# A relational graph attention layer with 23 instead of 24 buffers of gathered keys and values

## The chip, the cores and the metric

The kernel runs on one core of a Trainium2 chip. The metric is the device time of one execution in microseconds. Three runs took 1737.93, 1730.97 and 1749.97 us, median 1737.93.

## The reference

3125 nodes with 128 features and 100,000 edges, sorted by destination, each of one of five relations. For each relation every edge gets a query of its destination and a key and a value of its source (eight heads of 16), the attention is a softmax over the edges of one destination and one relation, and the weighted values are summed over edges and relations:

```
for r in range(5):
    mask = edge_types == r
    q = einsum(x[dst], W_Q[r]); k = einsum(x[src], W_K[r]); v = einsum(x[src], W_V[r])
    logits = (q * k).sum(-1) / 4 + attn_bias[r]
    m = segment_max(where(mask, logits, -1e9), dst)
    e = where(mask, exp(logits - m[dst]), 0)
    out += segment_sum(e / (segment_sum(e, dst)[dst] + 1e-12) * v, dst)
h = out @ out_proj_w.T + out_proj_b + x
y = x + layernorm(h) * ln_gamma + ln_beta
result = layernorm(y)
```

## The kernel before

**Tables.** A first stage (until some 120 us) multiplies the nodes by the five relations' weights and writes a table of keys and values to memory, `kv_d`, one row of 256 floats (1 KB) per node and relation. Queries go to `q_d`. A second path for inputs that don't fit the assumptions is compiled behind a test and not run.

**Groups and steps.** The edges are cut into 196 groups of 512, four edges on each of 128 partitions. A loop of steps k, written out in full with the order fixed by hand (lines 1123 to 1229), treats several groups at once at different points of their way. The first half of a group g runs in step g:

- `gather(g)`, line 698: four indirect DMAs issued by GpSimd, each 128 rows of `kv_d` into one of the four slots of the buffer `kvs_[g % KVB]`, with KVB = 24. Five groups (3, 6, 9, 12, 15) fetch their sources' features instead and multiply them on TensorE.
- `spread_q` (L803, TensorE) brings the queries of the group's window of nodes to its edges with 12 weight loads and 12 matmuls against a one-hot matrix `hot`.
- `logits` (L816 and L817, VectorE) multiplies queries by the gathered keys and sums per head; `store_logits` sends the logits to memory, `lg_d`.

**Maxima.** The nodes lie in 25 blocks of 128. When the last group that can hold an edge of a block has been through `logits` (about every eighth group), the step after issues `maxima_load` (L829): one indirect DMA on GpSimd, which fetches the logits of each node's edges out of `lg_d` into `ell`. It waits until the logits it needs have landed. `maxima` (L844 to L888: ScalarE once, then VectorE, in the steps three and four after that load's last group) makes the maxima, which go to memory and come back per group as `mw`.

**The second half** of group v runs in step `at_k[v]`, which the code works out from the blocks: v + 16 for the first seven groups, v + 18 for the next 15, v + 19 for all others. `spread_m` (L920, TensorE) brings the maxima to the edges, `less_max` (L929, VectorE) and `exps` (L933, ScalarE) make the exponentials, `weigh` (L938, VectorE) multiplies the gathered values by them, `sums` (L972, L974, L981, TensorE) adds over the edges of a node with a second one-hot matrix `at`. `norm` (L993 to L996, VectorE) divides, and projection, layer norms and output follow per block.

**Buffers.** The weighing is the last reader of a group's keys and values. So with 24 buffers the first DMA of `gather(g)` waits until VectorE has done `weigh` of group g - 24. The pool `hold` has 21 buffers of `hot` and `lg`, which live from before `logits` to `less_max`.

**Queues.** Each engine takes its instructions in the order of the program. In step k the program has, for GpSimd, `gather(k + 3)` and then, if a block is full, `maxima_load`; no other work stands on GpSimd in this part. Nothing ties GpSimd to a step but its waits: for the buffer, for the DMA that used the same semaphore eight DMAs ago, and, at L829, for the stored logits. In the last 16 steps the program has `gather(k + 1)` there. On VectorE a step is `weigh`, `less_max` of the next group, `norm`, `logits`, the one-hot matrix (L794), then maxima or layer norms where due. On TensorE it is `spread_m` of the next group, `sums`, `spread_q` of the next group.

Of the kernel before, what the change touches and what calls it, by code (L numbers as in the profile page):

```python
# [53 lines left out]
AHEAD = 3  # L54
# [6 lines left out]
SPAD = 5  # L61
XG = range(3, 16, 3)
QB = 3
KVB = 24
KVA = 9


# [1 line left out]
def gnn_kernel(  # L69
# [19 lines left out]
    with tc.manual_schedule():  # L89
        windowed_path(  # L90
            tc, n_bad_i, x, src, dst, edge_type, w_q, w_k, w_v, attn_bias, out_w, out_b,
            gamma, beta, out,
        )
# [39 lines left out]
def windowed_path(  # L133
# [5 lines left out]
    ctx = ExitStack()  # L139
# [34 lines left out]
    def buffers(those):  # L174
        for i in those:
            kvs_[i] = ctx.enter_context(tc.tile_pool(name=f"kvp{i}", bufs=1)).tile(
                [P, T, KVW], F32, name=f"kv{i}"
            )
# [508 lines left out]

    ps = ctx.enter_context(tc.tile_pool(name="ps", bufs=2, space=PSUM))
    buffers(i for i in range(KVB) if i not in at_once)
    hold = ctx.enter_context(tc.tile_pool(name="hold", bufs=KVB - AHEAD))  # L690
    flow = ctx.enter_context(tc.tile_pool(name="flow", bufs=2))
    late_flow = ctx.enter_context(tc.tile_pool(name="late_flow", bufs=2))
    def gather(g):
        if g in XG:
            return
        kv = kvs_[g % KVB]
        for t in range(T):
# [61 lines left out]
    def turn_x(g):  # L759
        xe = kvs_[g % KVB][:, :, H:]  # L760
        tx = ps.tile([P, T, P], F32, name="tx", tag="me")
        for t in range(T):
            nc.tensor.transpose(tx[:, t, :], xe[:, t, :], ident)
        live["tx", g] = tx
# [24 lines left out]
    def put_kv(g, t0):  # L789
        nc.scalar.copy(kvs_[g % KVB][:, t0 : t0 + 2, :], live.pop(("pk", g, t0)))  # L790

# [21 lines left out]
    def logits(g):  # L813
        kv, lg = kvs_[g % KVB], live["lg", g]
        prod = flow.tile([P, T, H], F32, name="prod", bufs=1)
        nc.vector.tensor_tensor(prod, kv[:, :, :H], live.pop(("qe", g)), op=ALU.mult)  # L816
        nc.vector.tensor_reduce(  # L817
            lg[:, :, :HEADS], prod.rearrange("p t (k d) -> p t k d", d=HD), AX.X, ALU.add
        )
# [915 lines left out]
```

## Time and profile before

| | |
|---|---|
| runs (median; lowest to highest) | 1737.93 us; 1730.97 to 1749.97 |
| profiled execution: device time | 1728.01 us |
| its span, first to last instruction | 1726.5 us |
| mean granted TensorE clock | 0.706 |
| PE busy (matmuls), PEld (weight loads) | 1030.0 us, 774.3 us |
| VectorE, ScalarE, GpSimd busy | 944.9, 640.4, 797.9 us |
| software queue (gathers, L829): share of 16 DMA engines | 22.5%, 112.08 MB |
| SP's hardware queue | 21.3%, 85.12 MB |

Times in a line of the timeline are the start and the duration in us, then engine, line, operation, the tiles written and read, how often, and in brackets the idle time before it on its engine and what ended it. "issue" means that the engine waited for nothing that the profile shows; "remote" and "another core or an unknown queue" that the profile can't name the releaser. GpSimd's "busy" counts the time in which it prepares and issues a DMA, not the transfer.

### The profile page before, as it was taken

How to read it: one execution, taken by the hardware profiler on the slowest of the kernel's cores; microseconds unless marked ns; L12 is line 12 of the kernel's file. 1: busy time of each engine (PE TensorE's matmuls, PEld its weight loads, DVE VectorE, ACT ScalarE, POOL GpSimd, SP SyncE). 2: the span in 40 equal slices, each digit the busy share in tenths (PEclk: the TensorE clock that was granted, in tenths of full speed). 3: DMA queues.
4: the chain of work that ended last, by engine and by line, in shares of the span. 5: the costliest groups of instructions: out<-in, count | busy, mean ns of one | idle time of the engine just before them, and what ended most of it. 6: DMA issues, size and time to landing. Idle time of an engine off the chain costs nothing.

```text
span 1726.5 us, 26128 instructions
## 1 busy us (share of the span) xinstructions
PE 1030.0 (60%) x7746; PEld 774.3 (45%) x7746; DVE 944.9 (55%) x2536; ACT 640.4 (37%) x2258; POOL 797.9 (46%) x901
## 2 busy tenths in 40 slices
PE   6874745345555546656755655665576556554676
PEld 2443524334444434434534544454454445443554
DVE  3552536345545554654754666466466646544776
ACT  1540103134334334333523434344343434442544
POOL 6344243355445445445454555536455553644300
PEclk8886966567667677666766666667676666757778
DMA  6773425245335445445544544544454443544410
GB/s 160 265 272 93 103 85 112 75 118 130 101 96 135 102 112 133 104 103 137 126 103 118 127 116 124 134 105 126 117 126 121 122 135 84 137 113 107 98 27 14
DMA packets 181946, 203.66 MB, mean 118 GB/s; under 512 B 83943, under 2 KB 146819, under 8 KB 181676
## 3 DMA queue, kind: packets, MB, share of 16 engines
q0 software_dynamic: 40576, 112.08, 22.5%
q1 hardware_dynamic: 136790, 85.12, 21.3%
q10 hardware_dynamic: 4430, 4.71, 1.1%
q8 instruction: 64, 1.05, 0.2%
q14 instruction: 86, 0.70, 0.1%
HBM read 166.51 MB, written 35.28 MB: 117 GB/s over the span
## 4 chain that ended last, share of the span: by engine, by line
PE 27%; DVE 27%; issue 18%; another core or an unknown queue 14%; ACT 5%; DMA 2%; SPq 1%; POOL 1%; DVEq 0%; ACTq 0%
PE pp L972 8%; PE qe L803 4%; DVE wl L867 4%; DVE mx L873 4%; DVE prod L816 4%; PE me L920 4%; PE pk L781 3%; DVE lg L817 3%; DVE wv L938 2%; PE pp L974 2%; PE pr L403 2%; ACT at L958 2%; DVE hot L794 2%; PE prq L724 1%
## 5 line engine op out<-in xcount | busy, mean ns | idle before, releaser
L698 POOL DMA_INDIRECT kv<-kv_d,idx x764 | 725.6, 950 | 503.0 <-DVE den L993 271.4
L972 PE MATMUL pp<-wv,at 128*125 128x136 f32 x1568 | 382.2, 374 | 83.6 <-issue 75.3
L972 PEld LDWEIGHTS pp<-wv,at 128*125 128x125 f32 x1568 | 286.7, 247 | 167.8 <-issue 159.1
L803 PE MATMUL qe<-qw,hot 125*128 125x128 bf16 x2352 | 228.9, 253 | 109.7 <-issue 98.3
L920 PE MATMUL me<-mw,hot 125*128 125x64 bf16 (+1 forms) x2352 | 142.3, 214 | 210.0 <-issue 110.5
L803 PEld LDWEIGHTS <-hot 125*128 125x128 bf16 x2352 | 197.6, 123 | 126.9 <-issue 112.1
L929 DVE TENSOR_TENSOR me<-lg,me 128x32 f32<-128x32 f32 x196 | 37.6, 192 | 374.6 <-remote 202.2
L958 ACT ACTIVATE at<-row_at,nkey 128x125 f32<-128x125 f32 x744 | 237.6, 398 | 0.0
L933 ACT ACTIVATE me<-me 128x32 f32<-128x32 f32 x196 | 35.7, 182 | 537.2 <-DVE me L929 451.2
L920 PEld LDWEIGHTS <-hot 125*128 125x128 bf16 x2352 | 123.4, 112 | 241.4 <-issue 191.4
L938 DVE TENSOR_TENSOR wv<-kv,me 128x512 f32<-128x512 f32 x196 | 132.9, 678 | 139.7 <-remote 85.9
L829 POOL DMA_INDIRECT ell<-lg_d,start_i x25 | 23.7, 946 | 303.2 <-DMA lg_d<-lg 87.3
L816 DVE TENSOR_TENSOR prod<-kv,qe 128x512 f32<-128x512 f32 x196 | 132.9, 678 | 43.6 <-PE qe L803 27.6
L974 PE MATMUL pp<-pt,carried 125*5 125x136 f32 x390 | 97.8, 339 | 68.4 <-issue 34.1
L817 DVE TENSOR_REDUCE lg<-prod 128x32 f32<-128x512 f32 x196 | 134.5, 686 | 6.8
L1006 ACT COPY oT<-pp 128x25 f32 x196 | 33.9, 173 | 245.6 <-remote 85.5
L961 ACT ACTIVATE at<-at 128x500 f32<-128x500 f32 (+1 forms) x196 | 117.4, 599 | 6.2
L724 PE MATMUL prq<-wq,xTq 128*128 128x384 f32 (+1 forms) x88 | 54.5, 718 | 94.3 <-DVE hot L794 77.8
L781 PE MATMUL pk<-wkv,xm 128*128 128x256 f32 x200 | 63.2, 447 | 50.7 <-issue 46.2
L867 DVE TENSOR_TENSOR wl<-by_head,shut 128x1536 f32<-128x1536 f32 (+2 forms) x49 | 73.1, 1491 | 36.0 <-PE pk L781 27.6
L981 PEld LDWEIGHTS pp<-rsum,o 125*128 125x128 f32 x392 | 80.5, 246 | 23.0 <-issue 22.2
L981 PE MATMUL pp<-rsum,o 125*128 125x25 f32 x392 | 71.9, 262 | 20.7 <-issue 16.1
(191 smaller groups left out, 1203.4 us busy)
## 6 DMA issues: line engine op xcount, KB each, us to landing
kt<-key_d SPq DMA_DIRECT2D x196, 128.0 KB
qw<-q_d SPq DMA_DIRECT2D x196, 96.0 KB
kv_d<-kvs SPq DMA_DIRECT2D x24, 640.0 KB
kv<-kv_d,idx POOLq DMA_INDIRECT x764
q_d<-q SPq DMA_DIRECT2D x22, 480.0 KB
lg_d<-lg SPq DMA_DIRECT2D x196, 18.0 KB
mw<-m_d SPq DMA_DIRECT2D x196, 6.0 KB
xr<-in_x SPq DMA_DIRECT2D x24, 64.0 KB
```

Of the source, the lines that this page charges most:

```text
L698: nc.gpsimd.indirect_dma_start(out=kv[:, t, :], out_offset=None, in_=kv_d[:, :], in_offset=bass.IndirectOffsetOnAxis(ap=idx[:, t, g : g + ...
L803: nc.tensor.matmul(qe[:, t, :], hot[:, t, :], qw[:WR, s, :], start=(s == 0), stop=(s == 2))
L816: nc.vector.tensor_tensor(prod, kv[:, :, :H], live.pop(("qe", g)), op=ALU.mult)
L817: nc.vector.tensor_reduce(lg[:, :, :HEADS], prod.rearrange("p t (k d) -> p t k d", d=HD), AX.X, ALU.add)
L867: nc.vector.tensor_tensor(wl, by_head[:, None].to_broadcast([P, n, nh, D]), shut[:, :n, None, :].to_broadcast([P, n, nh, D]), op=ALU.add,)
L920: nc.tensor.matmul(me[:, t], hot[:, t, :], mw[:WR, None, :, s, :].to_broadcast([WR, times, 2, HEADS // 2]), start=(s == 0), stop=(s == 2),)
L938: nc.vector.tensor_tensor(wv[:, :, :H].rearrange("p t (k d) -> p t k d", d=HD), kv[:, :, H:].rearrange("p t (k d) -> p t k d", d=HD), live ...
L958: nc.scalar.activation(at[:, t, :], row_at[:, :WR], AF.Abs, bias=nkey[:, t, g : g + 1], scale=1.0)
L961: nc.scalar.activation(at[:, on_dve:], at[:, on_dve:], AF.Relu, bias=1.0, scale=-1.0)
L972: nc.tensor.matmul(pp, at[:, t, :], wv[:, t, :], start=(t == 0), stop=(t == T - 1))
L974: nc.tensor.matmul(pp[:R], carried[:WR, g, :], live.pop(("pt", g - 1)), start=False, stop=False,)
L981: nc.tensor.matmul(op, live.pop(("o5", done)), rsum[:WR], start=True, stop=True)
```

## The change

The number of buffers of keys and values is 23, and the pool `hold`, whose size was worked out from it (24 - 3), keeps its 21.

```diff
-KVB = 24
+KVB = 23
+HELD = 21
 KVA = 9
...
     buffers(i for i in range(KVB) if i not in at_once)
-    hold = ctx.enter_context(tc.tile_pool(name="hold", bufs=KVB - AHEAD))
+    hold = ctx.enter_context(tc.tile_pool(name="hold", bufs=HELD))
```

Every use of a buffer (`gather`, `turn_x`, `put_kv`, `logits`, `weigh`) takes it as `kvs_[g % KVB]`. The first DMA of `gather(g)` so waits for `weigh` of group g - 23. No instruction is added, removed or put in another place of its engine's order.

## The prediction

> **What bounds the kernel now.** I read the page first: shares by engine, the chain that ended last, the costliest groups.
>
> ```profile
> PE 27%; DVE 27%; issue 18%; another core or an unknown queue 14%; ACT 5%; DMA 2%; SPq 1%; POOL 1%; DVEq 0%; ACTq 0%
> ...
> L698 POOL DMA_INDIRECT kv<-kv_d,idx x764 | 725.6, 950 | 503.0 <-DVE den L993 271.4
> ...
> L929 DVE TENSOR_TENSOR me<-lg,me 128x32 f32<-128x32 f32 x196 | 37.6, 192 | 374.6 <-remote 202.2
> ```
>
> No engine is full, and a third of the chain is "issue" or waits the profile can't name. GpSimd waits 271 us for VectorE: that is a gather waiting for its buffer (the line named, L993, follows the weighing, L938, on VectorE; the gather starts 0.3 us after the weighing ends). Does anyone wait for gathered data? From the view of line 816, the first reader, what ended VectorE's idle time before it:
>
> ```profile
>   DMA kv<-kv_d,idx: 0.6, 1
> ```
>
> Once, 0.6 us in 196 groups. So gathers are early enough; the question is what else they do. Next, the timeline. The starts of L816 show steps of 3 to 7.5 us, and about every eighth group one of some 22 us. Here is one, on GpSimd, TensorE and VectorE in turn:
>
> ```profile
> 920.69 0.95 POOL L829 DMA_INDIRECT ell<-lg_d,start_i  x1 [6.71 <-DMA lg_d<-lg]
> 921.94 0.95 POOL L698 DMA_INDIRECT kv<-kv_d,idx  x1 [0.30 <-issue]
> ...
> 940.75 0.94 POOL L698 DMA_INDIRECT kv<-kv_d,idx  x1 [0.30 <-issue]
> ```
> ```profile
> 939.05 0.26 PE L803 MATMUL qe<-qw,hot 125*128 125x128 bf16 x1 [1.12 <-issue]
> 940.44 0.27 PE L803 MATMUL qe<-qw,hot 125*128 125x128 bf16 x1 [1.13 <-issue]
> ...
> 944.64 0.58 PE L803 MATMUL qe<-qw,hot 125*128 125x128 bf16 x4 [1.11 <-issue]
> ```
> ```profile
> 927.17 0.68 DVE L938 TENSOR_TENSOR wv<-kv,me 128x512 f32<-128x512 f32 x1
> 944.84 0.20 DVE L929 TENSOR_TENSOR me<-lg,me 128x32 f32<-128x32 f32 x1 [16.98 <-remote]
> ```
>
> GpSimd was held 6.7 us at the load of logits (L829) and then issued 17 DMAs without a pause, one per 1.25 us. From 7 us into that run until 2 to 3 us after its end TensorE gets its instructions at multiples of 0.7 us ("issue": it waits for nothing recorded), and VectorE stands still for 17 us behind it. The same in busy time, columns PE, PEld, DVE, ACT, POOL, granted clock, DMA share, GB/s:
>
> ```profile
> 917.00:927.00 10.00, 7.34 (x89) 6.33 (x87) 8.65 (x27) 9.30 (x28) 4.79 (x6) 0.92 0.71 175
> 927.00:945.00 18.00, 4.83 (x21) 2.67 (x20) 1.02 (x5) 0.35 (x2) 11.34 (x12) 0.50 0.42 114
> ```
>
> The DMA engines are less busy in the stall (0.42) than before it (0.71), so it is not bandwidth. What tracks it is the run's length. In the GpSimd timeline I took as a run all issues with pauses under 0.6 us, and beside each summed TensorE's gaps over 0.6 us between starts, until 3 us after its end. Past 400 us: runs of 8 have 2.1 to 3.5 us of gaps, the two of 12 have 9.2 and 11.0, the eight of 13 have 12.4 to 14.2, the eleven of 17 have 18.8 to 20.9. Runs of 8 and 12 hold no load of logits, so that load is not the cause. Each further group (four DMAs) costs some 5 us. The trace gives a comparison for nothing, since runs after the load have 13 or 17 issues:
>
> ```profile
> 983.86 0.95 POOL L829 DMA_INDIRECT ell<-lg_d,start_i  x1 [6.84 <-DMA kt<-key_d]
> ...
> 998.88 0.95 POOL L698 DMA_INDIRECT kv<-kv_d,idx  x1 [0.30 <-issue]
> 1003.35 0.95 POOL L698 DMA_INDIRECT kv<-kv_d,idx  x1 [3.52 <-DVE den L993]
> ```
>
> This run stopped after three groups, because the fourth's buffer was not free. From one such load to the next: after 17 issues 62.6 us (mean of nine, 482 to 1286 us; 57.8 to 64.3), after 13 issues 58.4 us (five, 984 to 1401 us; 56.7 to 59.9). One more run of 13, at 736 us, was followed after 2.1 us by the next gather and took 64.0.
>
> **The change, part by part.** Instructions and their order stay as they are on all five queues; HELD keeps the hold pool at 21. What moves is one wait: the first gather of group g waited for the weighing of g-24, now g-23. In the steady part group v is weighed in step v+19, so a gather may start from step g-4 instead of g-5.
>
> The added wait, priced. Behind it on GpSimd stand the group's other three DMAs, the next groups, and every eighth group L829. Setting each gather to 0.3 us after the weighing it now waits for, with all else as traced, 110 of the 172 from group 24 on start later. Landing is 2.3 to 3.8 us after a group's last issue (bytes of the software queue counted in order). Slack from landing to L816 has a median of 31 us for groups 44 to 186 and becomes 26; the smallest in the steady part is 15.8. At the end groups 192 to 194 keep 11.0, 8.0 and 7.7, and 195 keeps its 1.2, since L829 holds it in both. Cost on the path: nothing, covered by these 8 to 30 us; if the cover failed, 5 us per group. L829's data land 3 us after issue and are read 26 us later (947 us), so up to 5 us of delay there is covered too.
>
> The DMA page of the Trainium skill (DMA: Bandwidth & Descriptors, Rules for kernel authors) speaks against the change: issue a DMA early, wait late. By that rule the sum could only be a loss, up to 5 us a group; the 0.6 us of L816 shows that this kernel is far past the point where earlier helps.
>
> What it saves. At a load of logits in step k, today's backlog is group k+4 (free since step k-1), then k+5, k+6, k+7 as weighings in steps k, k+1, k+2 end before the stall catches VectorE. With 23, k+7 needs the weighing of step k+3, behind the stall. In the run above, groups 102, 103 and 104 find buffers at 919.3, 922.3 and 927.9, but 105 only at 952.5. The eleven runs of 17 become 13: 11 x (62.6 - 58.4) = 46 us. Three longer early or late runs (33 at 283 us, 21 at 355 and 1575) lose one group by the same arithmetic: 3 x 5.0 = 15 us. The eight runs of 13 would become 9, but the moved group falls into the pause before L829: group 109, issued at 972.3, moves to 978.7 to 983.4 and meets the load at 983.9, so the run begins 5 us earlier and again has 13 issues. I take nothing there; bounds are 8 x 5 gained, or 2 us each lost because a 4-run stands 1.7 us before it (pauses of 1.6 and 1.2 us at 398 and 436 us left 2.7 and 3.5 us of gaps). Sum: about 60 us.
>
> The clock page (TensorE: Matmul & The Clock Gate, HAM oscillation) would blame the half clock that follows an idle array. The rows show 0.50 in the stall, but 12 matmuls of L803 take 0.83 us at full clock and 1.46 at half, against 9 us here; by that rule a shorter stall saves at most some 0.6 us x 22, 14 us in all.
>
> The profiled execution took 1728.0 us (span 1726.5), 10 below the median of the runs shown, 1737.9. 1728 - 60 = 1668 for such a run, 1678 on the median.
>
> **Rivals.** (a) *No change.* The stall is not caused by the run, or the same issues cost the same wherever they lie, and the group moved ahead of L829 gives all of it back. For it: the 64.0 us period, and 1.7 us pauses may not count as pauses. Against: TensorE's gaps begin some 6 us into a run and end within 3 us of its end, whatever its content. Time 1738, give or take 15.
>
> (b) *Slower.* Between the stall and the next load, gathers stand as 4, 4+4 and 4 issues with pauses of 2.3 to 2.8 us, which keep TensorE fed. Buffers freed one by one under 5.3 us apart would close them: an 8 becomes a 12, and gaps grow from 3 to 10 us, 7 per period. Nine such periods use up the 60 us, eleven or more show as a loss, all 20 make 140 - 60 = +80: 1818. For it: 12-runs at 1439 and 1501 us, in the faster steps at the end. Against: those pauses come from the maxima steps (7 us on VectorE), which stay.
>
> (c) *More than forecast.* All 22 loads lose a group outright, 110 us: 1628.
>
> (d) The change does nothing: excluded, as 110 gathers would have to wait longer.
>
> **How the numbers follow.** Forecast (3 to 4%) with what lies towards (c) 0.70, (a) 0.15, (b) 0.15. Runs of this kernel spread over 19 us, so 1%, 17 us, is what a measurement can tell: faster 0.70, same 0.15, slower 0.15. Range: 1635 leaves out the last of (c), 1750 takes in (a) and leaves out most of (b), about 2 in 10 together; without the rivals I would say 1655 to 1705.
>
> **What would show it.** After L829, 13 issues or fewer in every run, where 17 stood; L929's "remote" well below 202 us and the longest L816 steps near 16 us, not 22; 58 us from load to load; L816 still waiting under 5 us for gathers; GpSimd's wait on VectorE before L698 above 271. Wrong if runs of 17 remain across L829, if 12-runs appear between loads, or if the steps stay at 22 us with shorter runs.

## The result and the profile after

| | before | after |
|---|---|---|
| median of 4 runs each (lowest to highest) | 1739.14 us (1730.97 to 1749.97) | 1663.74 us (1658.07 to 1668.21) |
| profiled execution: device time, span | 1728.01, 1726.5 us | 1665.20, 1663.5 us |
| mean granted TensorE clock | 0.706 | 0.724 |

The ratio is 0.956, 95% interval 0.950 to 0.962: 75 us less, where 60 were forecast. (The two profiled executions differ by 63 us: the one before was quicker than its other runs.) That is so where these runs were taken. On two other chips the kernel before takes some 1220 us, and on the one of them where the changed kernel ran too, both take the same; the fifth experiment is about that.

Line numbers after the change are one higher (L698 is L699). The page and the groups by line of the changed kernel, for the lines that were shown of before:

```profile
PE 29%; DVE 28%; issue 19%; another core or an unknown queue 10%; ACT 5%; DMA 2%; SPq 1%; DVEq 0%; ACTq 0%; POOL 0%
...
L699 POOL DMA_INDIRECT kv<-kv_d,idx x764 | 724.5, 948 | 587.9 <-DVE den L994 346.6
...
L930 DVE TENSOR_TENSOR me<-lg,me 128x32 f32<-128x32 f32 x196 | 37.7, 193 | 348.6 <-remote 195.6
```

GpSimd's idle time behind VectorE before the gathers went from 271 to 347 us: the added wait. No reader of gathered data pays for it: the view of line 817, the first reader of gathered data, still has one wait:

```profile
  DMA kv<-kv_d,idx: 0.5, 1
```

L930's "remote" hardly moved (202.2 to 195.6 us), although its longest stalls shrank. The time went out of unnamed waits (the chain's share of them is 10% instead of 14%) and out of waits spread over other lines (L939's "remote" fell from 85.9 to 63.2 us).

Now a load of logits in the timeline. It is the same load of the program that stood at 983.86 us before, and the nearest in time to the one at 920.69 us. The bracket gives the idle time before the line on its engine:

```profile
925.01 0.95 POOL L699 DMA_INDIRECT kv<-kv_d,idx  x1 [0.30 <-issue]
926.71 0.94 POOL L830 DMA_INDIRECT ell<-lg_d,start_i  x1 [0.75 <-issue]
927.96 0.95 POOL L699 DMA_INDIRECT kv<-kv_d,idx  x1 [0.30 <-issue]
...
936.71 0.95 POOL L699 DMA_INDIRECT kv<-kv_d,idx  x1 [0.30 <-issue]
944.70 0.94 POOL L699 DMA_INDIRECT kv<-kv_d,idx  x1 [7.04 <-DVE den L994]
```
```profile
934.09 0.59 PE L804 MATMUL qe<-qw,hot 125*128 125x128 bf16 x4 [0.69 <-issue]
935.52 0.26 PE L804 MATMUL qe<-qw,hot 125*128 125x128 bf16 x1 [0.84 <-issue]
...
938.36 0.37 PE L804 MATMUL qe<-qw,hot 125*128 125x128 bf16 x2 [1.62 <-issue]
```
```profile
928.44 0.69 DVE L939 TENSOR_TENSOR wv<-kv,me 128x512 f32<-128x512 f32 x1 [1.72 <-PE me L921]
939.94 0.20 DVE L930 TENSOR_TENSOR me<-lg,me 128x32 f32<-128x32 f32 x1 [10.82 <-remote]
```

GpSimd issues the load and then two groups, nine issues, and stops for want of a buffer; before, three groups followed this load. The group ahead of it, 109, now ends 0.75 us before it instead of 6.85. TensorE's trickle is the same as before (gaps that end in "issue"), but shorter: 10 us of gaps in the run instead of 14. VectorE stands still for 10.8 us, where two stalls of 6.0 and 6.7 us stood at this load. At the load that had the stall of 17.0 us (at 920.69 us, now at 873.00), 8 gathers follow instead of 16, and the longest stall is 5.2 us.

Counted as in the prediction (a run ends at a pause of 0.6 us or more; beside it TensorE's gaps over 0.6 us between starts of matmuls or weight loads, until 3 us after its end), from 400 us on:

| | before | after |
|---|---|---|
| issues in a run that holds a load of logits | 11 x 17, 8 x 13, 1 x 21 | 2 x 17, 5 x 13, 12 x 9, 1 x 5 |
| TensorE gaps in the runs that hold a load | 354 us | 197 us |
| runs of 8 or more without a load; gaps in them | 17; 63 us | 26; 113 us |
| TensorE gaps in runs of 4 | 136 us | 170 us |
| mean time of eight groups, group 44 to 164 | 61.2 us | 58.6 us |

(The last two loads, in runs of five issues and one, are left out of the first line. Seven of the runs of 9 and one of 13 begin with the group that stands ahead of the load.) So 157 us of gaps went from the loads, and 83 of them came back in other runs.

### The profile page after: what moved, and what is told of

Read it like the earlier page. It is cut to its first block, busy times and chain, and to the rows that moved or that the text cites. A ratio compares the mean times of both kernels' runs of the same rounds, so it can differ in the third digit from the quotient of the medians.

```text
span 1663.5 us, 26129 instructions
## 1 busy us (share of the span) xinstructions
PE 1043.0 (63%) x7746; PEld 790.5 (48%) x7746; DVE 945.4 (57%) x2536; ACT 638.7 (38%) x2258; POOL 796.5 (48%) x901
## 4 chain that ended last, share of the span: by engine, by line
PE 29%; DVE 28%; issue 19%; another core or an unknown queue 10%; ACT 5%; DMA 2%; SPq 1%; DVEq 0%; ACTq 0%; POOL 0%
PE pp L973 9%; PE qe L804 4%; PE me L921 4%; DVE wl L868 4%; DVE mx L874 4%; DVE prod L817 4%; PE pk L782 3%; DVE wv L939 3%; DVE lg L818 2%; PE pp L975 2%; PE pr L404 2%; ACT at L959 2%; DVE hot L795 2%; PE prq L725 1%
## 5 line engine op out<-in xcount | busy, mean ns | idle before, releaser
L699 POOL DMA_INDIRECT kv<-kv_d,idx x764 | 724.5, 948 | 587.9 <-DVE den L994 346.6
L973 PE MATMUL pp<-wv,at 128*125 128x136 f32 x1568 | 392.7, 385 | 43.3 <-issue 34.1
L973 PEld LDWEIGHTS pp<-wv,at 128*125 128x125 f32 x1568 | 295.7, 256 | 122.4 <-issue 116.0
L804 PE MATMUL qe<-qw,hot 125*128 125x128 bf16 x2352 | 229.9, 256 | 87.7 <-issue 77.6
L804 PEld LDWEIGHTS <-hot 125*128 125x128 bf16 x2352 | 203.3, 125 | 99.6 <-issue 86.3
L921 PEld LDWEIGHTS <-hot 125*128 125x128 bf16 x2352 | 126.6, 113 | 253.5 <-issue 197.0
L934 ACT ACTIVATE me<-me 128x32 f32<-128x32 f32 x196 | 35.7, 182 | 542.0 <-DVE me L930 409.5
L930 DVE TENSOR_TENSOR me<-lg,me 128x32 f32<-128x32 f32 x196 | 37.7, 193 | 348.6 <-remote 195.6
L939 DVE TENSOR_TENSOR wv<-kv,me 128x512 f32<-128x512 f32 x196 | 133.0, 679 | 104.0 <-remote 63.2
L817 DVE TENSOR_TENSOR prod<-kv,qe 128x512 f32<-128x512 f32 x196 | 132.9, 678 | 43.2 <-PE qe L804 25.7
L975 PE MATMUL pp<-pt,carried 125*5 125x136 f32 x390 | 101.4, 350 | 57.8 <-ACT pt L988 27.4
```

Of the source, the lines that this page charges most:

```text
L699: nc.gpsimd.indirect_dma_start(out=kv[:, t, :], out_offset=None, in_=kv_d[:, :], in_offset=bass.IndirectOffsetOnAxis(ap=idx[:, t, g : g + ...
L804: nc.tensor.matmul(qe[:, t, :], hot[:, t, :], qw[:WR, s, :], start=(s == 0), stop=(s == 2))
L921: nc.tensor.matmul(me[:, t], hot[:, t, :], mw[:WR, None, :, s, :].to_broadcast([WR, times, 2, HEADS // 2]), start=(s == 0), stop=(s == 2),)
L939: nc.vector.tensor_tensor(wv[:, :, :H].rearrange("p t (k d) -> p t k d", d=HD), kv[:, :, H:].rearrange("p t (k d) -> p t k d", d=HD), live ...
L973: nc.tensor.matmul(pp, at[:, t, :], wv[:, t, :], start=(t == 0), stop=(t == T - 1))
L975: nc.tensor.matmul(pp[:R], carried[:WR, g, :], live.pop(("pt", g - 1)), start=False, stop=False,)
```

## The experiments

**1. Which weighing the gathers behind the load wait for: two kernels.** My theory: TensorE's supply of instructions dries up behind a long unbroken run of issues on GpSimd, and the change shortens the run behind each load. What decides the run's length is not the number of buffers but KVB - AHEAD, where AHEAD is the 3 in `gather(k + 3)`: the group placed in step k waits for the weighing of group k - 21 before and k - 20 after. The rival: fewer buffers help by themselves, with fewer transfers in flight. One kernel has 24 buffers and keeps the 20; the other has 23 and goes back to 21.

```diff
-AHEAD = 3        -AHEAD = 3
+AHEAD = 4        +AHEAD = 2
-KVB = 23          KVB = 23
+KVB = 24
```

> 24 buffers again, and AHEAD 4 instead of 3, so that in the program's order the load of logits (L830) stands behind gather(k + 4) and not gather(k + 3). Theory 1 (what counts is how many groups may be issued in one go behind the load): the first gather behind the load again waits for the weighing of its own step, as with 23 buffers and AHEAD 3, so runs behind the load are 9 to 13 issues and the time is that of 23 buffers, 1650 to 1680 us. Theory 2 (what counts is that gathers start later, nearer to their use, or that there are fewer buffers): gathers start as early as with 24 buffers before, time near 1739 us.

> 23 buffers as in the change, AHEAD 2 instead of 3: the load of logits stands behind gather(k + 2), so that one group more may follow it at once. Theory 1: runs of 17 behind the load return and with them the time of before, 1720 to 1760 us. Theory 2 (lead or number of buffers): 23 buffers stay, gathers start no earlier, time near 1664 us.

Measured, beside 1742.67 us for the kernel before on the chip of these runs: with 24 buffers and 20, 1681.63 us, ratio 0.964 (0.955 to 0.973), 2 us above the expected range; with 23 buffers and 21, 1738.66 us, 0.997 (0.992 to 1.001). The second has its runs of 17 back (12 of the 15 loads between groups 44 and 164, with 17.9 to 20.6 us of gaps), and the 16 us stall:

```profile
927.38 0.94 POOL L699 DMA_INDIRECT kv<-kv_d,idx  x1 [0.30 <-issue]
928.63 0.95 POOL L699 DMA_INDIRECT kv<-kv_d,idx  x1 [0.30 <-issue]
940.79 0.94 POOL L699 DMA_INDIRECT kv<-kv_d,idx  x1 [11.21 <-DVE den L994]
```
```profile
915.80 0.69 DVE L939 TENSOR_TENSOR wv<-kv,me 128x512 f32<-128x512 f32 x1 [0.63 <-issue]
932.84 0.20 DVE L930 TENSOR_TENSOR me<-lg,me 128x32 f32<-128x32 f32 x1 [16.36 <-remote]
```

The first has 5, 9 and 13 there (2, 6 and 7 times). So the number of buffers is not it; the place of the gathers and the load against the weighing is.

Another rival is that transfers pile up in a long run. The kernel before's own trace speaks against it: counting the packets of the software queue in order, a gather lands 3.0 to 3.8 us after its issue (medians) for the first four gathers behind the load in its runs of 17, and 2.4 us for the last eleven, while TensorE starves. Where there is no stall (experiment 5) the median is 3.3 us.

**2. The load one step later.** 23 buffers as in the changed kernel, and each `maxima_load` one step further down, so that another group stands ahead of it.

```diff
-            if full_step[b] + 1 == k:
+            if full_step[b] + 2 == k:
```

> 23 buffers, AHEAD 3, and the load of logits issued one step later (at full_step + 2), behind one more gather; its logits have then landed, so GpSimd should not be held there at all. Theory 1: no backlog forms, runs of at most 8 or 9 issues, TensorE's gaps in the step after the load nearly gone, 8 to 9 us less per period: 1580 to 1650 us. Theory 2: no change, 1655 to 1675 us. A rival to both: the maxima, read three steps after the block is full, now wait for the load, 3 to 6 us per block, 1680 to 1760 us.

1645.37 us, ratio 0.943 (0.936 to 0.950). Between groups 44 and 164 the runs behind a load are 13 times 9 and twice 13, and eight groups take 58.3 us. So the runs of 9 did not vanish, and the steady part is hardly quicker than the changed kernel's (58.6): the 8 to 9 us per period that were expected did not come. Group 44 is reached 11 us earlier than there and the last group 21 us earlier; most of what it gains on the changed kernel lies ahead of the steady part and behind it.

**3. Pauses instead of buffers.** 24 buffers as before, and six memsets of a spare tile on GpSimd behind each gather.

```diff
+        for _ in range(6):
+            nc.gpsimd.memset(idle, 0.0)
```

> 24 buffers, AHEAD 3 as before, and after each gather six short memsets on GpSimd of a tile that nobody reads, some 2 us in all, so that the same backlog is issued with pauses. Theory 1 (an unbroken run starves TensorE): gaps in TensorE behind the load shrink from 19 to 21 us to a few us though the same four groups follow; a group then takes 7 us of GpSimd, 57 us per eight, so the time is 1640 to 1710 us. Rival (the backlog itself, its DMAs in flight or its bytes, is what costs): gaps as before, 1739 us or more.

1632.16 us, ratio 0.936 (0.929 to 0.942), the lowest of all on this chip, though this kernel gives GpSimd 362 us more to do. It lies below the expected 1640 to 1710. Behind the first stage no run is longer than 5 issues. The gaps in the runs that hold a load fell from 354 to 29 us; these runs are shorter too, so all gaps are the better measure. From 130 us on, TensorE's gaps over 0.6 us that end in "issue" sum to 493 us in the kernel before, 387 in the changed one and 79 here; those that end with ScalarE or VectorE rise from 262 us before to 578 here. From the timeline and the groups by line of this kernel:

```profile
705.61 0.95 POOL L701 DMA_INDIRECT kv<-kv_d,idx  x1 [0.30 <-issue]
706.54 2.18 POOL L706 MEMSET idle<- 128x256 f32 x6
709.11 0.94 POOL L701 DMA_INDIRECT kv<-kv_d,idx  x1 [0.39 <-issue]
```
```profile
L821 DVE TENSOR_TENSOR prod<-kv,qe 128x512 f32<-128x512 f32 x196 | 133.6, 682 | 205.2 <-DMA kv<-kv_d,idx 185.9 <-PE qe L808 10.9 <-PE tx L768 5.9
...
L934 DVE TENSOR_TENSOR me<-lg,me 128x32 f32<-128x32 f32 x196 | 37.6, 192 | 135.7 <-PE me L925 55.6 <-PE pj L1019 19.3 <-PE pp L986 17.7
```

"remote" is gone from L934's leading waits, and a new one takes its place: 185.9 us for gathers at L821. A group now takes GpSimd 709.11 - 701.85 = 7.26 us, and eight groups take 60.4 us, hardly less than before (61.2). Most of the gain lies ahead of the steady part: group 44 is reached at 409 us instead of 507. On this chip, then, the stall needs issues that follow each other closely: the same issues with pauses between the groups do not make it. (The pauses also make the issues fewer per us, and no run here separates the two.)

**4. Fewer buffers, shorter pauses, fewer bytes: on another chip.** Four kernels: 22 buffers with `gather(k + 2)` (20 again); three memsets behind each gather; six behind every second one; and 24 buffers whose gathers fetch half rows (this kernel leaves the values out). The second and third diff are against experiment 3, the others against the changed kernel; the half rows also have 24 buffers and a memset of the values, not shown.

```diff
-AHEAD = 3
+AHEAD = 2
-KVB = 23
+KVB = 22
```

> 22 buffers and the program's lead shortened by one group again, so that the same number of buffers (20) lies between a gather's place in the program and the weighing it waits for as in the changed kernel; gathers run at most two to three groups ahead. Theory 1 (what counts is which weighing the gathers behind the load wait for, not how far they run ahead): runs behind the load as in the changed kernel, 9 and 13, no more than two of 17, a period of 58 to 60 us, 1650 to 1690 us. Rival (a short lead is itself what helps: 17-runs are gone with any shorter lead): the one with 23 buffers and the same program lead would have been fast too, which it was not. Rival (a short lead costs: gathers land too late): VectorE waits over 30 us for gathers at L817 and the time is 1700 us or more.

```diff
-        for _ in range(6):
+        for _ in range(3):
```

> 24 buffers, three memsets of a spare tile on GpSimd (about 0.36 us each, 1.1 us together) behind each gather instead of six. GpSimd then needs 8 x (5.0 + 1.1) + 1.25 = 50 us per eight groups and is no longer the bound, as it was with six (7.25 us a group, 59.7 us from load to load). Theory 1: no run over 5 issues; if a pause of 1.1 us lets TensorE recover, its steady period falls below 59 us, VectorE waits less than 100 us for gathers, and the time is 1590 to 1630 us. Rival (1.1 us is too short: in the kernel before, pauses of 1.2 and 1.6 us left 2.7 and 3.5 us of gaps): gaps of 3 to 10 us within chains of such groups, time 1640 to 1700 us. Rival (it is not the run but the DMAs in flight): no better than the changed kernel, 1650 to 1680 us.

```diff
-        for _ in range(6):
+        for _ in range(6 if g % 2 else 0):
```

> 24 buffers, six memsets (2.17 us) on GpSimd behind every second gather. GpSimd needs 8 x 5.0 + 4 x 2.17 + 1.25 = 50 us per eight groups, as with three behind each. Theory 1: no run over 9 issues; each run of 8 leaves 2 to 4 us of gaps, which TensorE makes up in between or not: period 56 to 59 us, 1590 to 1640 us, within 20 us of the version with three memsets behind each. Rival (any pause works alone by slowing GpSimd down): the same time as the version with three within 10 us, with TensorE gaps per run no smaller than before.

```diff
-                out=kv[:, t, :], out_offset=None, in_=kv_d[:, :],
+                out=kv[:, t, :H], out_offset=None, in_=kv_d.rearrange("n (s c) -> (n s) c", s=2),
```

> 24 buffers and the kernel before's order; each gather fetches rows of 512 bytes instead of 1 KB (the first half row only, from other rows than the index means; the values are zero). This changes what is computed: the values are left out and the keys are other ones. The number of gather instructions, their order and their waits are those of the kernel before. Theory 1 (the length of GpSimd's unbroken run of issues starves TensorE, whatever the DMAs move): runs of 17 issues after most loads again, with 17 to 21 us of TensorE gaps, a period of 60.5 to 62 us per eight groups, 1715 to 1750 us. Rival (the bytes of the gathers, or DMA bandwidth, hold TensorE up): the gaps of a run of 17 shrink to some 10 us, and the time falls by at least 60 us.

These expectations were written for a chip that shows the stall, and this one doesn't: the kernel before took 1220.82 us here (1216.66 to 1229.62, 13 runs). 22 buffers: 1225.23 us, ratio 1.002 (0.999 to 1.004). Three memsets: 1416.49 us, 1.159 (1.154 to 1.164). Six at every second: 1410.65 us, 1.154 (1.149 to 1.160). Half rows: 1215.61 us, one run. The pauses cost what they last: 191 gathers by three memsets of 0.36 us are 206 us, and the times rose by 196 and 190. So with pauses GpSimd sets the pace on this chip. Whether the stall depends on the gathers' bytes remains unmeasured, since there was no stall here to change.

**5. The change itself on that chip.**

> The changed kernel once more, because on the last chip the kernel before took 1220.8 us instead of 1740: there GpSimd issued up to 297 gathers without a pause while TensorE had its matmuls of L804 in 0.83 us for twelve, and the period was 41.4 us, which is GpSimd's own 8 x 5.0 + 1.25. Theory 1, now narrower (the change saves the stall that TensorE has behind long runs, where a chip shows that stall): if the kernel before takes some 1740 us on this chip, the changed one takes 1650 to 1685 us; if the kernel before takes some 1220 us, there is no stall to save and the ratio is 0.995 to 1.01. Rival (a shorter lead helps by something else, say fewer transfers in flight): 3 to 5% faster on either kind of chip.

> Half rows again (values left out, keys from other rows, 24 buffers and the order of the kernel before), to have it on a chip that shows the stall. If the kernel before takes some 1740 us here: theory 1 (the run of issues, not the bytes) says 17-runs with 17 to 21 us of gaps and 1700 to 1750 us; the rival (bytes or DMA bandwidth) says gaps of some 10 us and less than 1680 us. If the kernel before takes some 1220 us, this one does too, within 10 us, and nothing is told apart.

The changed kernel took 1219.56 us, the kernel before 1221.65: ratio 0.9995 (0.996 to 1.003). Half rows again took 1215.68 us. The profile of the changed kernel there, first its engines and the clock, then the gathers and L930, to be set against 724.5 and 348.6 above:

```profile
PE 880.4 (72%) x7746; PEld 691.0 (57%) x7746; DVE 949.8 (78%) x2536; ACT 639.5 (53%) x2258; POOL 800.4 (66%) x901
...
PEclk9897997779778787877888688778788877777787
...
L699 POOL DMA_INDIRECT kv<-kv_d,idx x764 | 727.4, 952 | 246.8 <-issue 192.0 <-DMA kv_d<-kvs 13.5 <-DVE prod L817 7.6
L930 DVE TENSOR_TENSOR me<-lg,me 128x32 f32<-128x32 f32 x196 | 37.4, 191 | 103.7 <-PE me L921 100.3 <-issue 1.6 <-PE qe L804 0.9
```

An issue takes GpSimd the same 0.95 us. The clock's row has mostly 7 and 8, where before it had 6 and 7. Nothing is "remote" at L930, and GpSimd hardly waits for VectorE before a gather. Here it is in the timeline, near the end of a run of 132 issues:

```profile
705.47 0.94 POOL L699 DMA_INDIRECT kv<-kv_d,idx  x1 [0.30 <-issue]
706.72 0.95 POOL L699 DMA_INDIRECT kv<-kv_d,idx  x1 [0.30 <-issue]
```
```profile
702.44 0.83 PE L804 MATMUL qe<-qw,hot 125*128 125x128 bf16 x12
...
705.93 0.83 PE L804 MATMUL qe<-qw,hot 125*128 125x128 bf16 x12
```

The longest run has 182 issues and lasts 228 us, and TensorE gets its 12 matmuls of L804 in 0.83 us inside such runs; in the profile with the stall, above, they were strewn over 7 us. Eight groups take 42.1 us, against 8 x 4 x 1.25 + 1.25 = 41.25 us of issuing. So GpSimd sets the pace here without pauses too. With it behind, the buffer is nearly always free when a gather comes to it, so the moved wait has nothing to hold back.

**6. The later load and the half rows on a third chip.**

> 23 buffers with the load of logits one step later, once more. On a chip where the kernel before takes some 1740 us: 1630 to 1660 us as before. On one where it takes some 1220 us: GpSimd's issues are the same in number and it never waits for long, so 1210 to 1235 us, a ratio of 0.99 to 1.01; that would make it a version that gains where the stall is and costs nothing where it isn't. If the later load is on the path there (ScalarE and VectorE waited 158 and 128 us for its data in the version with three memsets on such a chip), up to 2 us per load, 40 us, ratio 1.03.

> Half rows a third time (values left out, keys from other rows, 24 buffers and the order of the kernel before), in the hope of a chip that shows the stall. Where the kernel before takes some 1740 us: theory 1 (the run of issues, not the bytes) says 17-runs with 17 to 21 us of gaps and 1700 to 1750 us; the rival (bytes or DMA bandwidth) gaps of some 10 us and less than 1680 us. Where it takes some 1220 us, within 10 us of it again and nothing is told apart.

The kernel before took 1216.36 us. The later load: 1230.85 us, ratio 1.013 (1.011 to 1.016), a small loss, outside the 0.99 to 1.01 that were expected where the load is not on the path. Its data come late: ScalarE (L845) and VectorE (L853) waited 28.0 and 26.9 us for `ell` instead of 4.1 and 3.3 in the changed kernel of experiment 5, and gathers 41.0 us for buffers. Half rows: 1211.90 us.

Of the versions that gain most where the stall is, the later load loses 1.3% where it isn't; of the pauses, the shorter ones of experiment 4 lost 15 to 16%, and six behind each were not tried there.

## Why the prediction was right, and where its terms were off

The time (1663.7) lies in the range and within 15 us of the forecast, by the mechanism that was named. The terms, each as how far ahead of before the changed kernel is at successive loads; they add up to the 62.8 us by which the last load is ahead, and the spans differ by 63.0. Neighbouring periods trade with each other (8.9 us gained follow 2.4 lost), so the sums are firmer than single periods:

| what stands there before | forecast | measured |
|---|---|---|
| up to the load at 414 us (33, 33 and 21 issues) | 10 us | 13.4 us |
| eleven periods that begin with 17 issues | 46 us | 58.4 us |
| eight periods that begin with 13 issues | 0 | -7.2 us |
| from the load at 1575 us (21 issues) to the last | 5 us | -1.8 us |

That the sum comes so near (62.8 against 61) is partly luck: the terms miss by 3, 12, -7 and -7 us, and these cancel.

- **17 becomes 13: it did, and often went further.** Behind each of these loads stood four groups, 16 gathers, without a pause. Now 16 follow once, 12 three times, 8 five times and 4 twice. So in ten of eleven the fourth group fell behind the stall, as forecast, and in seven of these others fell with it. In all ten the group ahead of the load in the program is issued later too: it ends 0.3 to 3.4 us before the load, where 5.9 to 11.5 us lay. The prediction worked that out for the 13s alone. A period gained 5.3 us, not 4.2. The step that was off is the arithmetic with each gather set to its new wait "with all else as traced".
- **13 stays 13: right ahead of the load, wrong behind it.** In six of the eight the group ahead of the load now adjoins it, as worked out for group 109. Here the last gather of group 77, the load, the last gather of 78 and the first of 79:

```profile
692.59 0.95 POOL L699 DMA_INDIRECT kv<-kv_d,idx  x1 [0.30 <-issue]
693.84 0.95 POOL L830 DMA_INDIRECT ell<-lg_d,start_i  x1 [0.30 <-issue]
...
698.84 0.95 POOL L699 DMA_INDIRECT kv<-kv_d,idx  x1 [0.30 <-issue]
702.86 0.94 POOL L699 DMA_INDIRECT kv<-kv_d,idx  x1 [3.08 <-DVE den L994]
```

But one group follows these loads without a pause, where two were forecast and three stood before: 4 + 1 + 4 makes 9 issues, not 13. (109 itself ends 0.75 us before its load, with two groups behind it; one load keeps its three.) What was lost came after: in five of the six a run of 8 now starts some 3 us behind the 9, with 4.2 to 6.3 us of gaps, where a run of 4 with 0 to 3.6 us stood. That fits the loss, though no run measures it alone. The prediction named 2 us lost in each such period as a bound and took nothing; it was 0.9.
- **The early part was right, the late one not.** The run of 33 at 283 us lost two groups and the one of 21 one, 13 us in all. The run of 21 at 1575 became 17, but its period took 62.1 us in both.
- **Rival (b) came true in part.** No 12 stands between loads in the steady part, but runs of 8 rose from 15 to 22 between groups 44 and 164: from 400 us on 83 us of gaps came back in runs without a load, against 157 saved behind loads. Rival (c), 110 us, did not come.
- **The slack held.** From landing to first reader the groups 44 to 186 have a median of 24.8 us (26 forecast) and at least 15.7 us (15.8 forecast).
- **The signs.** GpSimd's wait above 271 us, gathers under 5 us at L817: right. "13 or fewer in every run": two runs of 17 remain, at 401 and 1510 us. Longest steps "near 16": between groups 44 and 164 the longest is 18.5 us instead of 23.0, and 8 steps are over 12 us where 12 were. 58 us from load to load: right (58.6 for eight groups). L930's "remote" well below 202: wrong, since the name covers more than the long stalls; the single stall was the better sign.
- **What the prediction did not see** is that its central row, 5 us of stall per further group, is not a property of the run alone: on two other chips it is not there. Nothing in the one profile could show this; its text says "what tracks it is the run's length", and where the stall is, experiments 1 and 3 bear this out.

## What to carry to other kernels

When one long wait holds a queue, count what is free to go the moment it ends; the buffers upstream set the size of that burst, and moving the wait by one group can matter more than a buffer. A lead that no reader uses up can be given away: here the later issue gained 4.4% on one chip and was neutral, 0.9995, on another. (The Trainium skill, DMA: Bandwidth & Descriptors, Rules for kernel authors, asks for issuing early and waiting late. The changed kernel's gathers, which still land 25 us ahead of their reader on the one chip and 10 us on the other (medians), don't show it; the load of logits of experiment 6, whose data came late, does.) Before a kernel is tuned to a stall, see whether the stall is there on a second chip: pauses cured it on the first, and shorter ones cost up to 16% on the second.

## What was not expected of the hardware

The kernel before takes some 1740 us where the result and the first three experiments were measured, and 1220 us on two other chips. No chip was seen in both conditions, so whether the chip itself makes the difference, or something around it at the time, is not shown. The work of VectorE and GpSimd differs little: in the changed kernel VectorE is busy for 945.4 and 949.8 us, and an issue on GpSimd takes 0.95 us on both. TensorE's matmuls are busy for 1043.0 and 880.4 us, at granted clocks of 0.72 and 0.81. What differs is TensorE's supply: starts that lie 0.6 to 1.6 us behind the one before come 429 times in the changed kernel with the stall and 77 times without; of these, 331 and 4 end in "issue".

What starves TensorE stays open. It is not late refill by the instruction queues, as far as the records go: around the run at 983.9 us of the kernel before (13 issues, 14.2 us of gaps) no packet of either instruction queue lies between 3 us before it and 4 us behind it. (Of the runs of 13 or more from 200 us on it is the only such one; around the others lie one to four packets.) The Trainium skill (Runtime: NRT & Kernel Launch, Instruction fetch mechanics) calls the cost of crossing a 16 KiB boundary of instructions mostly hidden; this row does not speak against it. Single packets take about the same with the stall (the kernel before) and without (22 buffers): the median of 16 KB of instructions is 972 and 991 ns, of 4 KB of gathered rows 159 and 159. A run of issues on GpSimd is needed for the stall on the chip of experiments 1 to 3, since pauses remove it, but it is not enough, since in experiment 5 a run of 182 leaves TensorE alone. What adds the rest was not found.
